# A graph kernel on one core: instruction order from a table of engine clocks, the second eight of a neighbour list from a code counted from the far end, and weighted slots summed by TensorE

## The chip, the cores and the metric

The kernel runs on one core of one Trainium2 chip. The metric is the time of one execution in microseconds on the device; the median of three runs without the profiler is given. A core has TensorE (PE in the profile: matmuls; PEld: its weight loads), VectorE (DVE), ScalarE (ACT), GpSimd (POOL), SyncE (SP: it only issues transfers here) and 16 DMA engines. Each engine works off its own instruction stream in order.

## The reference

There are 16 graphs of 1024 nodes with 64 features per node and a dense adjacency `adj` (16 x 1024 x 1024, float32). An entry is set with about 1.6% chance, and the diagonal is set. Four layers follow, each with a residual and a layer norm:

```
x = LN(x + tanh([x, adj @ x] @ W1 + b1) @ W2 + b2)          # layer 0
x = LN(x + (adj / max(rowsum(adj), 1)) @ x)                 # layer 1
for weights in (L2, L3):                                    # layers 2 and 3
    nb   = (adj > 0) without the diagonal;  m = nb.sum(-1)
    skip = ceil(m / 2) where m > 10                         # remove two neighbours of a node ...
    rem  = nb & ((rank + 1) % skip == 0);  rem |= rem.T     # ... and the reverse edges
    valid = (nb without rem) plus the node itself
    agg  = 0.25 q(0.25) + 0.5 q(0.5) + 0.25 q(0.75)         # quantiles, channel by channel, of x over the
    x    = LN(x + (relu((x + agg) @ V1 + c1) @ V2 + c2) * mask)   #   valid neighbours, interpolated
```

The quantiles are the heart: for every node, the features of its neighbours are gathered and sorted in each of 64 channels, and a few of the sorted slots are weighed and summed.

## The kernel before, in words

**Lists.** For each graph ("entry" `b`) the function `features` does layers 0 and 1 and makes `near`, the 0/1 adjacency in fp8. `lists` then works in steps. It counts the neighbours with TensorE (`pm`), finds ranks with a triangular matrix (`pr`), finds the two places to cut with ScalarE's Sign and an accumulator, marks them (`takes`), subtracts them and their transposes (`pv`), and counts what is left. It sorts the nodes by their count, so that a tile of 128 nodes has lists of like length: `order` is the permutation as a matrix. For each of the tiles 0 to 6 (`SIZES` 10, 11, 13, 14, 15, 17, 19 with the node itself) it multiplies `order` by the rest of `near` (`pk`), so that each neighbour appears as a code that falls with its new position, and takes the codes with VectorE: MAX8 gives the eight largest, MATCH_REPLACE8 strikes them out, MAX8 gives the next eight. The codes become indices `idx`.

**Gathering and sorting.** `ordered` permutes features and helper data. Graphs go in pairs; 16 rounds (`order_of_rounds`) are 8 pairs times the layers 2 and 3. For tiles 0 to 6 GpSimd gathers one list slot of 128 nodes with one indirect DMA (`gather`, L373) into a ring of `ROOM` = 60 slots for each of the pair's two graphs (`got_s`). `exchange` sorts the slots with VectorE min and max operations between `got_s` and `other`. `weigh` multiplies the wanted slots by weights on ScalarE (L850), adds them in a tree on VectorE and adds the two last into `agg`. The tile with the longest lists (half 21, half 33 slots) is not gathered: `fill` picks its neighbours with TensorE. For each slot a 0/1 mask `hot` is made from `place` (three of four by VectorE, the fourth by ScalarE at L808 and L809), and 24 matmuls (`pick`, L369) select rows into `pgk`, whose groups of four slots ScalarE copies to `got` (L800). `finish` does the small MLP of the round: transposes (`pt`, L886), two matmuls and a layer norm.

**Order.** VectorE, ScalarE and TensorE run exactly in the order in which the Python program emits their instructions (a manual schedule). All steps are generators. The class `Metered` adds up an estimated time for every VectorE instruction; a step yields a number, written by hand, of VectorE microseconds that should pass before it continues, and `Weave.catch_up`, called after every sorting operation, lets every due step emit its instructions:

```python
def step(self, work):
    try:
        work[0] = max(self.now() - work[2], work[0]) + work[3] * next(work[1])
```

Gathers are tried at the same moments (`fetch`), and only when the whole list of an entry is ready. All VectorE instructions of this part carry line 212 in the profile (the helper that counts them).

Of the kernel before, what the change touches and what calls it, by code (L numbers as in the profile page):

```python
# [12 lines left out]
F32 = mybir.dt.float32  # L13
# [16 lines left out]
KS = -(-(max(SIZES[:LISTED]) - 1) // 8) * 8  # L30
# [4 lines left out]
HOTS = 6  # L35
# [162 lines left out]
class Metered:  # L198


    def __init__(self, engine):
        self.engine, self.us = engine, 0.0

    def __getattr__(self, name):
        call = getattr(self.engine, name)

        def counted(*args, **kwargs):
            aps = [a for a in (*args, *kwargs.values()) if hasattr(a, "shape") and hasattr(a, "dtype")]
            size = max(prod(a.shape[1:]) for a in aps)
            fast = name == "tensor_scalar" and all(mybir.dt.size(a.dtype) == 2 for a in aps if prod(a.shape[1:]) > 1)  # L210
            self.us += 0.13 + size / (3840 if fast else 960)
            return call(*args, **kwargs)  # L212

        return counted
# [3 lines left out]
def adj_resnorm_kernel(ctx: ExitStack, tc: tile.TileContext, x, adj_t, nodemask, w01, b01, w02, b02,  # L218
# [10 lines left out]
    dve = Metered(nc.vector)  # L229
# [6 lines left out]
    make_identity(nc, ident)  # L236
# [16 lines left out]
    nc.gpsimd.iota(minus_k, pattern=[[-1, KW]], base=0, channel_multiplier=0, allow_small_or_imprecise_dtypes=True)  # L253
    one_f = const.tile([P, 1], F32, name="one_f")
# [27 lines left out]

    def per_row(ap, name):
        t = const.tile([P, C], F32, name=name)
        nc.sync.dma_start(t, ap.rearrange("(o c) -> o c", o=1).to_broadcast([P, C]))
        return t

    def column(ap, name):
# [4 lines left out]
        (weight(w21, "w21s"), column(b21, "b21c"), weight(w22, "w22s"), per_row(b22, "b22r")),  # L293
        (weight(w31, "w31s"), column(b31, "b31c"), weight(w32, "w32s"), per_row(b32, "b32r")),
# [87 lines left out]
    def settle(dst, y, chain):  # L382
# [4 lines left out]
        yield 2  # L387
# [3 lines left out]
        yield 9  # L391
        dve.reduce_sum(st[:, 2], dst, axis=AX.X)
        yield 1
        nc.scalar.activation(st[:, 3], st[:, 2], AF.Sqrt, bias=eps, scale=1.0 / C)
        yield 6
        dve.reciprocal(st[:, 0], st[:, 3])
        yield 1
        for t in range(NT):
            nc.scalar.activation(dst[:, t, :], y[:, t, :], AF.Copy, scale=st[:, 0, t : t + 1])
        yield 7  # L400

    def split(xc, parts, rest):

        yield 1
        nc.scalar.copy(parts[:, :, 0, :], xc)
        yield 6
        dve.tensor_sub(rest, xc, parts[:, :, 0, :])
        yield 1
        nc.scalar.copy(parts[:, :, 1, :], rest)
        yield 6  # L410
        dve.tensor_sub(rest, rest, parts[:, :, 1, :])
        yield 1
# [4 lines left out]
    def features(b, e):  # L417
# [11 lines left out]

        load(0)  # L430
# [4 lines left out]
        yield 8  # L435
        for h in range(NH):

            node_in = s.work.tile([P, HALF], F32, name="node_in", bufs=1)
            px = s.psum.tile([P, HALF], F32, name="px", tag="x", bufs=1)
            for q in range(G):  # L440
                nc.tensor.transpose(px[:C, q * P : (q + 1) * P], x_s[:, h * G + q, :], ident)
            for q in range(G):
                t = h * G + q
                for jt in range(NT):
# [4 lines left out]
                yield 5  # L449
                load(t + 2)  # L450
            yield 5
            nc.scalar.copy(node_in[C:], px[C:])
            yield 3
            nc.tensor.matmul(px[:C], w01s, node_in, start=True, stop=True)
            yield 9
            hid_t = s.work.tile([C, HALF], F32, name="hid_t", tag="node_in", bufs=1)
            nc.scalar.activation(hid_t, px[:C], AF.Tanh, bias=b01c)
            yield 3
# [3 lines left out]
            yield 10  # L462
# [3 lines left out]
        while b >= 2 and not entries[b - 2].packed:  # L466
            yield 2
        near = s.sets.tile([P, NT, N], F8, name="near", bufs=2)
        for h in range(NH):
            pa = s.psum.tile([P, G, C + 1], F32, name="pa", tag="x", bufs=1)  # L470
            for q in range(G):
                i = NT + h * G + q
                t = i - NT
                rows = slice(t * P, (t + 1) * P)
                for jt in range(NT):
                    nc.tensor.matmul(pa[:, q, :], adj[i][:, jt, :], x1[:, jt, :], start=jt == 0, stop=jt == NT - 1)  # L476
                yield 4
                dve.tensor_scalar(near[:, :, rows], adj[i], 0.0, None, op0=ALU.is_gt, saturate=False)
                dve.tensor_tensor(near[:, t, rows], near[:, t, rows], ident_b, op=ALU.is_gt, saturate=False)
                load(i + 2)  # L480
            yield 8
# [4 lines left out]
        e.near = near  # L486
        x2 = s.feat.tile([P, NT, C], F32, name="x2", tag="x_s", bufs=1)
        dve.tensor_add(y, y, x1[:, :, :C])
        yield from settle(x2, y, "x")
        while b and entries[b - 1].xs[0] is None:  # L490
            yield 2
# [4 lines left out]
    def lists(b, e, pace):  # L496

        while e.near is None:
            yield 2
        near = e.near  # L500

        st = s.work.tile([P, 6, NT], F32, name="nb_st", bufs=1)
# [3 lines left out]
        pm = s.psum.tile([P, N], F32, name="pm", tag="big", bufs=2)  # L506
# [3 lines left out]
        yield 12  # L510
        nc.scalar.copy(m, pm[:, :NT])
        yield 5
# [10 lines left out]
        for t in range(NT + 1):  # L523
            if t < NT:
                pr = s.psum.tile([P, N], F32, name="pr", tag="big", bufs=2)
                prs.append(pr)
# [5 lines left out]
            yield 1.2  # L532
            if t:
                for i in range(2):
                    junk = s.work.tile([P, N], F16, name="junk", tag="dist", bufs=3)
                    nc.scalar.activation(junk, prs[t - 1], AF.Sign, bias=lim[:, i, t - 1 : t], scale=-1.0,  # L536
                                         accum_out=cut_at[:, i, t - 1 : t])
            yield 3
        yield 5
# [5 lines left out]
        dve.tensor_scalar(off, off, 0.25, None, op0=ALU.mult)  # L545
        while b and not entries[b - 1].placed:
            yield 2
        takes = s.sets.tile([P, NT, N], BF, name="takes")
        dists = []
        for t in range(NT + 2):  # L550
# [3 lines left out]
            yield 1.3  # L554
            if t >= 2:
                dve.tensor_scalar(takes[:, t - 2, :], dists[t - 2], off[:, t - 2 : t - 1], None, op0=ALU.is_equal)
# [11 lines left out]
        yield 3  # L568
        for t in range(NT + 1):
            if t < NT:  # L570
                rows = slice(t * P, (t + 1) * P)
                pv = s.psum.tile([P, N], F32, name="pv", tag="big", bufs=2)
                pvs.append(pv.rearrange("p (c n) -> p c n", n=P))
# [7 lines left out]
            yield 1.2  # L581
            if t:
                nc.scalar.activation(left(t - 1), pvs[t - 1], AF.Relu, saturate=False)
# [31 lines left out]
        for t in range(NT):  # L615
            dve.tensor_scalar(order[:, t, :], slot, key[:, 2, t : t + 1], None, op0=ALU.is_equal)
            if t % 3 == 2:
                yield 2
# [795 lines left out]
```

## Time and profile before

| | |
|---|---|
| median of 3 runs | 5103.43 us (5102.24 to 5104.99) |
| profiled execution | 6960.85 us, of which 6959.1 us from the first to the last instruction |
| VectorE | 4338.6 us busy, 9272 instructions |
| GpSimd | 3219.1 us busy; 2944 gathers of 1045 ns and 128 stores of rows of 1060 ns |
| TensorE | 4047.0 us busy in 44,824 matmuls; mean granted clock 0.69 |
| ScalarE | 2838.3 us busy, 6388 instructions |
| DMA | 255.23 MB, mean 37 GB/s |

The profiled execution is much longer than a run without the profiler. A row of the costliest groups gives the line, the engine, the operation, output <- inputs, shapes and count, then busy us and mean ns, then the idle time of the engine just before these instructions and what ended it. A row of the waits gives who waited, for what, total us, times, and the longest.

### The profile page before, as it was taken

To read this page: it belongs to the slowest core of one execution; us is meant where nothing else is said; L and a number is where in the kernel's file an instruction comes from. 1 tells how busy PE (TensorE), PEld (TensorE's weight loads), DVE (VectorE), ACT (ScalarE), POOL (GpSimd) and SP (SyncE) were. 2 spreads that over 40 slices of the span, in tenths; PEclk is the share of its full clock that TensorE was granted. 3 is DMA by queue.
4 is the path that set the end of the run, shared out by engine and by line. 5 is a ranking of instruction groups with operands and counts; after the bars stand their busy time and mean duration, and the time that the engine had idled before them with its cause. 6 is when DMAs were issued, how large, how long until landed. Compare 5 with 4: busy or idle time off the path is not lost.

```text
span 6959.1 us, 112002 instructions
## 1 busy us (share of the span) xinstructions
PE 4047.0 (58%) x44824; PEld 2895.5 (42%) x44824; DVE 4338.6 (62%) x9272; ACT 2838.3 (41%) x6388; POOL 3219.1 (46%) x3168
## 2 busy tenths in 40 slices
PE   6757657386557665666666566665756563333243
PEld 5435435254334443444445344443534443223232
DVE  2446537577647668485665858566574767557575
ACT  4336335354344445344433535334353443223232
POOL 0342225625453545454454644455453645665551
PEclk8778777597668766767676667766667675555555
DMA  3111102111111111111111111111111100000100
GB/s 87 46 44 50 49 24 49 40 48 42 46 31 40 43 43 35 36 45 32 43 41 41 37 34 44 32 43 40 43 34 27 34 18 22 21 21 17 22 19 6
DMA packets 416527, 255.23 MB, mean 37 GB/s; under 512 B 104554, under 2 KB 366842, under 8 KB 415994
## 3 DMA queue, kind: packets, MB, share of 16 engines
q1 hardware_dynamic: 317690, 147.12, 7.7%
q0 software_dynamic: 98304, 100.86, 6.8%
q8 instruction: 352, 5.77, 0.3%
q14 instruction: 181, 1.48, 0.1%
HBM read 235.18 MB, written 12.59 MB: 36 GB/s over the span
## 4 chain that ended last, share of the span: by engine, by line
PE 34%; DVE 28%; issue 20%; another core or an unknown queue 8%; ACT 7%; POOL 1%; DMA 1%; DVEq 0%; ACTq 0%; POOLq 0%
PE pgk L369 11%; DVE other L212 11%; DVE got_s L212 7%; PE pk L640 6%; DVE got L212 5%; PE pa L476 4%; PE px L445 2%; PE ordered_x L369 2%; PE pr L530 1%; ACT got_s L850 1%; PE pk L632 1%; POOL got_s L373 1%; DVE hot L212 1%; PE pk L638 1%
## 5 line engine op out<-in xcount | busy, mean ns | idle before, releaser
L373 POOL DMA_INDIRECT got_s<-table,idx x2944 | 3075.3, 1045 | 3514.5 <-issue 784.3
L369 PEld LDWEIGHTS <-hot 128*128 128x128 bf16 x24576 | 1092.7, 112 | 1821.9 <-issue 1488.7
L369 PE MATMUL pgk<-x0p,hot 128*128 128x64 bf16 x12288 | 655.0, 212 | 694.6 <-issue 517.1
L369 PE MATMUL pgk<-x1p,hot 128*128 128x64 bf16 x12288 | 664.4, 216 | 646.5 <-issue 407.4
L800 ACT COPY got<-pgk 64x256 f32<-64x256 f32 x416 | 151.9, 365 | 1976.7 <-PE pgk L369 1352.4
L212 DVE TENSOR_SCALAR hot<-place 128x1024 bf16<-128x1024 f16 x768 | 332.0, 435 | 730.2 <-remote 518.2
L640 PE MATMUL pk<-near,order 128*128 128x512 fp8e4 x1792 | 495.9, 419 | 56.2 <-issue 54.0
L212 DVE TENSOR_TENSOR other<-got_s 128x512 f32<-128x512 f32 (+9 forms) x850 | 507.7, 608 | 29.8 <-ACT got_s L1035 15.3
L212 DVE TENSOR_TENSOR got_s<-got_s 128x512 f32<-128x512 f32 (+9 forms) x867 | 483.6, 560 | 18.4
L530 PE MATMUL pr<-steps,near 128*128 128x512 bf16 x1536 | 420.2, 436 | 96.8 <-ACT junk L536 72.5
L476 PE MATMUL pa<-x,adj_r 128*128 128x65 f32 x2048 | 359.7, 332 | 165.7 <-issue 156.9
L850 ACT ACTIVATE got_s<-got_s,wts 128x64 f32<-128x64 f32 x1568 | 393.8, 335 | 79.6 <-DVE got_s L212 70.7
L476 PEld LDWEIGHTS pa<-x,adj_r 128*128 128x128 f32 x2048 | 344.1, 251 | 177.5 <-issue 166.9
L212 DVE TENSOR_TENSOR got_s<-other 128x512 f32<-128x512 f32 (+9 forms) x731 | 401.2, 562 | 9.5 <-DVE other L212 1.5
L212 DVE TENSOR_TENSOR other<-other 128x384 f32<-128x384 f32 (+10 forms) x617 | 322.3, 522 | 17.1
L651 ACT ACTIVATE code<-pk 128x1024 f16<-128x1024 f32 x112 | 114.2, 1020 | 511.7 <-PE pk L640 344.5
L212 DVE MAX8 best<-code 128x8 f16<-128x1024 f16 x240 | 293.8, 1224 | 45.3 <-ACT code L651 32.3
L445 PE MATMUL px<-adj_r,x_s 128*64 128x128 f32 x2048 | 291.6, 299 | 47.4 <-issue 35.0
L640 PEld LDWEIGHTS <-order 128*128 128x128 bf16 x1792 | 167.3, 103 | 327.2 <-issue 197.4
L536 ACT ACTIVATE junk<-pr,nb_st 128x1024 f16<-128x1024 f32 x256 | 281.6, 1106 | 52.0 <-remote 21.8
L530 PEld LDWEIGHTS <-near 128*128 128x128 fp8e4 x1536 | 165.6, 110 | 327.9 <-issue 199.4
L809 ACT ACTIVATE hot<-hot,one_f 128x1024 bf16<-128x1024 bf16 x256 | 293.9, 1148 | 12.7 <-remote 4.4
(215 smaller groups left out, 7095.5 us busy)
## 6 DMA issues: line engine op xcount, KB each, us to landing
adj_r<-in_adj_dram SPq DMA_DIRECT2D x256, 512.0 KB
got_s<-table,idx POOLq DMA_INDIRECT x2944
x_s<-in_x_dram SPq DMA_DIRECT2D x16, 256.0 KB
table<-x2s SPq DMA_DIRECT2D x16, 256.0 KB
table<-x3s SPq DMA_DIRECT2D x16, 256.0 KB
out_dram<-agg,out_rows POOLq DMA_INDIRECT x128
table<-no_row SPq DMA_DIRECT2D x12, 0.2 KB
w01s<-in_L_gnn_W_dram SPq DMA_DIRECT2D x1, 32.0 KB
```

The source lines that it names most:

```text
L212: return call(*args, **kwargs)
L369: nc.tensor.matmul(dst, hot[:, c, :], parts[:, c, q, :], start=first and c + q == 0, stop=c == NT - 1 and q == 2)
L373: nc.gpsimd.indirect_dma_start(out=dst, out_offset=None, in_=tab, in_offset=bass.IndirectOffsetOnAxis(ap=rows, axis=0))
L445: nc.tensor.matmul(px[C:, q * P : (q + 1) * P], x_s[:, jt, :], adj[t][:, jt, :], start=jt == 0, stop=jt == NT - 1)
L476: nc.tensor.matmul(pa[:, q, :], adj[i][:, jt, :], x1[:, jt, :], start=jt == 0, stop=jt == NT - 1)
L530: nc.tensor.matmul(pr[:, h * HALF : (h + 1) * HALF], near[:, c, t * P : (t + 1) * P], steps[:, ONSET + h * HALF - c * P :][:, :HALF], star ...
L536: nc.scalar.activation(junk, prs[t - 1], AF.Sign, bias=lim[:, i, t - 1 : t], scale=-1.0, accum_out=cut_at[:, i, t - 1 : t])
L640: nc.tensor.matmul(cols, order[:, c, rows], left(c, slice(h * G, (h + 1) * G)), start=False, stop=c == NT - 1)
L651: nc.scalar.activation(codes[done], pks[done], AF.Relu, scale=float(N))
L800: nc.scalar.copy(got[rows, waiting[0] : waiting[0] + 4, :], waiting[1][rows])
L809: nc.scalar.activation(by_act, by_act, AF.Relu, bias=one_f, scale=-1.0)
L850: nc.scalar.activation(got[:, m, i, :], got[:, m, slot_id, :], AF.Copy, scale=e.wts[:, t, i : i + 1])
```

## The change

**Order.** `Metered` and all yielded numbers go. `Clocks` keeps one clock per engine and, for blocks of 128 bytes, when they were last written and read. Every emitted instruction (`Timed` wraps all engines) is priced, starts in this model once its engine is free and its inputs are there, and moves the clocks. A step yields nothing (it comes again 0.3 us after its last result, or polls every 0.5 us) or the model time at which it wants to go on; `Weave.run` always takes the earliest. Steps ask the model before they emit: `landed` (inputs written), `vacant` (buffer free), `big` (one of two PSUM buffers read out), `hot_room`. `fetch` and the sorting become steps of their own; a gather may be issued once its own tile is listed. `lists` is cut in two (`cuts` and `lists`); making the `hot` masks (`mark_picks`) is apart from the picking (`fill`); a finished tail list is sorted as soon as it is filled. For entries 0 to 3 `near` is marked in the first pass over the adjacency (layer 0) and not in the second.

```diff
-class Metered: ...
+class Clocks:
...
+    def put(self, engine, name, args, kwargs):
...
+        took, late = self.cost(engine, name, out, ins)
+        start = max(self.free[engine], self.now)
...
+                    start = max(start, end if by == engine else seen)
...
+        end = self.free[engine] = start + took
...
+        def run(self):
+            while self.works:
+                work = min(self.works, key=lambda w: (w[0], w[1]))
+                clocks.now, clocks.last = max(clocks.now, work[0]), 0.0
...
+                if at is None:
+                    at = clocks.last + SLACK if clocks.last else clocks.now + POLL
...
+    def landed(*aps):
+        while clocks.when(*aps) > clocks.now:
+            yield clocks.when(*aps) + SLACK
```

In `features` (where `first` is `b < 4`), `fetch`, `exchange` and `fill`:

```diff
+                if first:
+                    mark(t)
...
-            for i in range(1, SIZES[t]):
-                gather(got[:, m, i, :], ...)
+                for i in range(1, SIZES[t]):
+                    yield from quiet("POOL", 3.0)
+                    gather(got[:, m, i, :], ...)
...
         for is_max, d, v, i, j, to in usual[t]:
+            ins = view(pair[i], v), view(pair[j], v, d)
+            while max(clocks.free["DVE"], clocks.when(*ins)) > clocks.now:
+                yield max(clocks.free["DVE"], clocks.when(*ins))
...
-            weave.catch_up()
-            fetch()
+            yield clocks.now
...
+            while True:
+                at_least = max(clocks.when(hot), clocks.free["PE"] - (SLACK if k < 2 else 4.0), clocks.unused(pg) if place == 0 else 0.0)
+                if at_least <= clocks.now:
+                    break
+                yield at_least
```

Picks are copied out in groups of `GROUP` = 3 slots instead of 4; there are `HOTS` = 5 mask buffers instead of 6.

**Second eight.** ScalarE makes two codes of a tile instead of one: one that is large for the first neighbours, one that is large for the last. Lists of 9 to 16 neighbours need one MAX8 on each and no MATCH_REPLACE8; the list of 18 takes two on the near end and one on the far end. Where both cover a neighbour twice, a comparison drops the second.

```diff
-                    nc.scalar.activation(codes[done], pks[done], AF.Relu, scale=float(N))
+                    nc.scalar.activation(codes[done][0], pk, AF.Relu, bias=ends_of[:, 0:1], scale=2.0 * N)
+                    nc.scalar.activation(codes[done][1], pk, AF.Abs, bias=ends_of[:, 1:2], scale=2.0 * N)
+                    nc.scalar.activation(codes[done][1], codes[done][1], AF.Relu, bias=ends_of[:, 2:3], scale=-1.0)
...
-                size = -(-links // 8) * 8
-                for k in range(0, size, 8):
-                    dve.max(best[:, k : k + 8], rest)
-                    if k + 8 < size:
-                        dve.match_replace(rest, best[:, k : k + 8], rest, 0.0)
+                firsts = -(-(SIZES[done] - 1) // 8) - 1
+                for k in range(firsts):
+                    dve.max(best[:, k], near_end)
+                    if k + 1 < firsts:
+                        dve.match_replace(near_end, best[:, k], near_end, 0.0)
+                dve.max(best[:, 2], far_end)
...
+                dve.scalar_tensor_tensor(signed[:, most:links], best[:, 2, : links - most], signed[:, KS : KS + 1], rest,
+                                         op0=ALU.is_gt, op1=ALU.mult)
```

**Sums.** The weighted slots and the node's own features are summed by TensorE, which multiplies each by the identity and accumulates in `acc`, a strip of 128 columns in PSUM; one tile at a time (`adding`); the constant `HALVINGS` of the code below is 0, so that no add of the tree is left. The sum is transposed by this, so `finish` needs no transposes; ScalarE copies it to `agg`. The count of neighbours left now comes from the accumulator of the Relu that writes them, so a second ScalarE pass is gone.

```diff
-        while left > 2:
+        for _ in range(HALVINGS):
             more = left // 2
             dve.tensor_add(...)
             left -= more
-        if t < LISTED:
-            dve.tensor_add(agg[:, which, t, :], prods[:, :, 0, :], prods[:, :, 1, :])
...
+        while adding:
+            yield
+        adding.add(k)
...
+            for i in range(left):
+                nc.tensor.matmul(acc[own, rows], prods[:, i, :], ident[:, rows], start=i == 0, stop=False)
+            nc.tensor.matmul(acc[own, rows], e.xs[layer][:, at, :], ident[:, rows], start=False, stop=True)
         free.add((k, t, present))
         free.add((k, t))
+        yield
...
+            nc.scalar.copy(agg[own, at, :], acc[own])
+        adding.remove(k)
...
-        dve.tensor_add(agg, agg, xc)
...
-                nc.tensor.transpose(pt[:C, q * P : (q + 1) * P], agg[:, h * G + q, :], ident)
...
-                nc.scalar.activation(left(t - 1), pvs[t - 1], AF.Relu, saturate=False)
-                nc.scalar.activation(junk, left(t - 1), AF.Sign, accum_out=key[:, 4, t - 1 : t])
+                nc.scalar.activation(left(t - 1), pv, AF.Relu, accum_out=key[:, 4, t - 1 : t], saturate=False)
```

## The prediction

> **What bounds the kernel now.** I read the busy line first, then the costliest groups of VectorE and GpSimd, then their waits, then single stretches.
>
> The head of the page, the busy time of each engine:
>
> ```profile
> span 6959.1 us, 112002 instructions
> PE 4047.0 (58%) x44824; PEld 2895.5 (42%) x44824; DVE 4338.6 (62%) x9272; ACT 2838.3 (41%) x6388; POOL 3219.1 (46%) x3168
> ```
>
> Under the profiler no engine is full. But the median without it is 5103.43 us, 1857 us less than the profiled 6960.85 us, for the same instructions. Operations don't get shorter because nobody looks (a VectorE operation of 512 floats takes 687 ns here, and that is its slope and fixed cost, see below), so what is missing from the timed runs is idle time. In a timed run VectorE is then busy 4338.6 / 5103 = 85%, and at most 765 us idle.
>
> GpSimd looks lighter than it is. Its gathers, in order of time:
>
> ```profile
> 2058.42 0.94 POOL L373 DMA_INDIRECT got_s<-table,idx  x1 [0.31 <-issue]
> 2059.66 0.94 POOL L373 DMA_INDIRECT got_s<-table,idx  x1 [0.30 <-issue]
> ...
> 2083.10 1.39 POOL L373 DMA_INDIRECT got_s<-table,idx  x1 [0.31 <-issue]
> ```
>
> Start to start is 1.24 us although 0.94 is called busy: each gather brings 0.30 us of issue. With the mean of 1045 ns it is 1.345 us a gather. There are 2944 gathers and 128 stores of rows: 3072 x 1.345 = 4132 us, 81% of the timed run. So two engines share the bound, and each feeds the other. GpSimd's waits show how:
>
> ```profile
> POOL got_s L373 <- issue: 784.3, 2434, 25.7
> POOL got_s L373 <- DVE other L212: 764.3, 86, 87.9
> POOL got_s L373 <- DVE got_s L212: 676.1, 104, 29.5
> POOL got_s L373 <- ACT got_s L850: 617.9, 103, 23.3
> ...
> POOL got_s L373 <- DVE code L212: 193.7, 1, 193.7
> ```
>
> The 764, 676 and 618 us are gathers that wait for room in the ring: sort, weighing and adding of an older tile are not done. The last line is the start: the first gather goes out at 202.35 us. VectorE's own longest waits:
>
> ```profile
> DVE hot L212 <- remote: 518.2, 48, 61.7
> DVE y_m L212 <- PE pd L899: 241.1, 30, 28.5
> DVE hot L212 <- PE pgk L369: 200.7, 49, 19.9
> DVE deg L212 <- PE pa L476: 172.2, 14, 56.8
> ```
>
> These are waits of source order: a `hot` mask stands in VectorE's stream before a buffer is free, and sorts that could run stand behind it. TensorE is late there partly because of the profiler (`PEld L369 <- issue` 1595 us, `PE pgk L369 <- issue` 925 us, waits for nothing on record), which I take for most of the 1857 us.
>
> **What the Trainium skill says.** "VectorE: DVE Perf Modes", section on the TRN2 errata, gives a float32 `tensor_tensor` of N elements (N+151)/0.96 ns, 691 for 512; the trace has 687 to 691 and 292 for 128, so it agrees, and I price removed adds with it. "TensorE: Matmul & The Clock Gate", Part 1, has two clocks, 1.2 and 2.4 GHz; the trace agrees: 32 matmuls `px` L445 take 3.65 us (114 ns each) at one place, while 256 of `pt` L886 keep TensorE busy 55.5 us (217 ns each). "ScalarE: Activation LUTs", section on ACT_TABLE_LOAD, gives 280 + 0.833 N ns for an activation with a pointer bias, 1133 at 1024; the trace has 1144 and 1148 (`hot`), 1106 from PSUM.
>
> **The change part by part.** Counts are from the built instruction lists of both kernels.
>
> *Sums to TensorE.* VectorE loses 238 adds `got_s<-got_s` with 71,700 elements, (71,700 + 238 x 151)/960 = 112 us; 96 `got<-got` with 24,600 elements, 41; the 119 + 64 adds into `agg`, 31 + 3 + 14 = 48; 32 adds `agg+x` of 512, 22. The MLP's bias adds become 128 of half width, +10. Sum -213 us.
> TensorE gains 1792 float32 matmuls of 128 columns for seven tiles of a list (1568 slots, 224 own rows) and 928 of 64 columns for the tail: at 114 to 217 ns and half of it 204 + 53 to 389 + 101 us, less 256 transposes (29 to 56): +230 to +435 us on 4047. TensorE isn't the bound: its dense pieces run far below its mean (144 `ordered_x` in 4.20 us, 29 ns each; 24,576 `pgk` at that rate are 713 us, on record at 1319). Hidden beside VectorE, except for order, see the rivals.
>
> *Second eight from the other end.* MATCH_REPLACE8 goes from 128 to 16: 112 x (1209 + 92 ns for its value load) = -146 us. MAX8 stays 240. 112 small comparisons come, at 179 ns (a 128x8 row) +20. Sum -126 us. ScalarE pays: two more passes over 1024 per tile, 112 x (1106 + 1148 ns) = 252, 336 small copies at some 0.24 us 80, evacuations of the sums 50, copies by three instead of four 25; it loses 128 `junk` passes, -135, and the `o_t` copies, -37. About +240 us on 2838: 3080, 60 to 67% of any run forecast here, hidden.
>
> *VectorE in all:* -213 - 126 = -339 us, 4339 to 4000. GpSimd: nothing, 4132.
>
> *Order.* The order by summed VectorE time and written lags goes; each step is now placed when a table of engine clocks says that its inputs have landed. That moves everything, masks and matmuls included; mask making is now a task of its own, ahead of the matmuls. SP's adjacency loads and table writes move with it: the 256 loads wait for `px` in the SP queue (1805 us there), cost nothing where three buffers cover it, and would show as `px` waits on DMA if they came late; 1.2 us do today. Gathers may start per listed tile rather than per whole list. For entries 0 to 3 the `near` marks move to the first pass, so two stretches of 14 us (`pa` L476) leave the path to the first gather. On VectorE the marks stand before the adds of the first layer; those wait 0.7 us a mark, 8 x 0.7, which the loads cover. With five instead of six `hot` buffers a mask can wait one pick (24 matmuls of 29 ns, 0.7 us) more; from below nothing, from above 768 x 0.7 / 2 = 270 us if half did.
> The 765 us of idle time, split by the trace: some 150 of the first 200 us (VectorE is busy 50 us in the first two stretches of 100) and some 70 at the end (93 busy of the last 160) belong to the ends, 545 to the middle. I let the start fall to 110, the end to 60. For the middle nothing in the trace of before gives the answer: bounds 0 and 545, and I take half, 270.
>
> VectorE then ends at 4000 + 110 + 60 + 270 = 4440. GpSimd has its own sum: first gather at 165, 4132 of gathers, some 85 from the last gather to the end, 4382 with no stall at all. Two chains this even delay one another: the ring holds 60 slots, a round needs 99. I add 5% of the gathers, 200 us: **4580 us**. Against the profiled run: its VectorE was idle 2620 us, most of it the profiler's; the profiled span should fall by about the 339 us of work plus waits, to some 6100 to 6600, but I don't wager on that.
>
> **The rivals.**
> *Work alone.* The order gains nothing, since the waits only change their names: 5103 - 339 = 4764. For it: half the `hot` waits come from late TensorE, and order doesn't speed that. Against: y_m, deg, own waits are pure order.
> *Gathers alone.* The order is so good that GpSimd never stalls: 4132 + 202 + 100 = 4434, or less if a gather costs less unprofiled. For it: 2058 us of ring waits in the trace, which such an order aims at. Against: the ring keeps its size.
> *Slower: the one strip of sums.* All sums go through a single strip of PSUM, one tile at a time, and stand in TensorE's one stream behind `pk` groups and `pv` steps that wait for ScalarE (`PE pv L576 <- ACT near L583`: 143.6 us in 28 waits, up to 35.8). Ring room is given back only after the sum, so a gather waits for TensorE where it waited for an add of VectorE. There are 119 + 32 such sums. The gain of 339 us is gone once each holds the ring 339 / 151 = 2.2 us longer on the path; at 3 us it is 4764 + 453 = 5217. An add tree takes 213 / 151 = 1.4 us today, a sum of two members 16 x 0.217 = 3.5 us plus its place in the queue, so the point is within reach if the ring is the limit all the time and the order brings nothing.
> *No difference.* Less VectorE work is filled by waits for gathers and TensorE: 5100. That needs both engines idle at 20% with a better order, unlikely. That the change doesn't do what it says is ruled out by the instruction lists: the adds and 112 replacements are gone.
>
> **How the numbers follow.** Forecast 4580 (chance 0.43), work alone 4764 (0.24), gathers alone 4434 (0.20), slower by the strip 5217 (0.10), same 0.03. A measurement can tell about 0.2% here. Faster 0.87, same 0.03, slower 0.10. The range takes in the first three with the bounds of the middle's idle time and the `hot` buffers: from just under 4434 to 4764 plus half the 270, 4380 to 4900; 0.13 lies in the other two cases, and the rest beyond its ends.
>
> **What would show it.** VectorE busy 4000 +- 40 us on some 8,760 instructions; MATCH_REPLACE8 x16; gathers x2944 at the same 1.05 us; TensorE busy 4280 to 4480, ScalarE about 3080. The first gather before 170 us. `hot` waits of VectorE well below 730 us, and GpSimd's waits for `other`, `got_s` below 2058. If instead GpSimd waits mostly for the sums on TensorE, the strip has decided; if VectorE's busy time stays above 4200 my prices are wrong; if the busy time falls and the time doesn't, the order is.

## The result, and the profile after

The kernel after takes 5039.09 us (median of 4 runs, 5028.11 to 5056.69) beside 5103.78 us for the kernel before: a ratio of 0.9877 (95% interval 0.9848 to 0.9905), 65 us faster. The forecast was 4580 us, 459 us too low, and the result lies above the whole range of 4380 to 4900.

One thing is needed to read the numbers: the kernel before takes 5104 to 5106 us on some chips and 6988 to 7110 us on others. Its profile, of 6960.85 us, shows what chips of the second kind show; its times and the profile of the kernel after are those of the first kind.

This is the head of the page of the kernel after. The rows of digits show 40 equal slices of the span: tenths of busy time for three engines, and the granted TensorE clock in tenths of full speed.

```profile
span 5035.1 us, 123964 instructions
...
PE 3791.2 (75%) x50028; PEld 3000.9 (60%) x50200; DVE 4018.0 (80%) x8678; ACT 3079.9 (61%) x7175; POOL 3312.4 (66%) x3168
...
PE   6887988887888787888788777888878675563532
...
DVE  2568558897898978888888987988798888879593
...
POOL 0436217776377775777667675777757776777774
PEclk9989987898999888889899888888988887776765
```

The profiled execution took 5036.86 us, as long as the others, so profiling costs this kernel next to nothing. The work of two engines came out as forecast: VectorE 4018 us on 8678 instructions (4000 on 8760), ScalarE 3080 (3080). TensorE's 3791 us lie below the forecast of 4280 to 4480; that is at least in part the kind of chip, as a kernel run on both kinds shows below. VectorE is idle for 5035 - 4018 = 1017 us, where the forecast's sum for VectorE left it 440, and the 4580 us left it 580. TensorE, which was called "not the bound", is at least 70% busy in every slice from the 2nd to the 31st.

Rows of the costliest groups (busy us, mean ns; then the idle time before them):

```profile
L300 POOL DMA_INDIRECT got_s<-table,idx x2944 | 3165.2, 1075 | 1629.4 <-issue 509.9 <-DMA got_s<-table,idx 219.7 <-DVE other L300 179.8
L300 PE MATMUL pgk<-ident,got_s 128*64 128x128 f32 x3136 | 423.5, 311 | 226.8 <-ACT got_s L300 177.3 <-ACT got L300 46.3 <-ACT agg L300 3.0
L300 PE MATMUL pgk<-ident,got 128*64 128x64 f32 x1792 | 140.6, 254 | 180.1 <-ACT got L300 146.7 <-DVE takes L300 33.5
L300 ACT COPY agg<-pgk 128x128 f32<-128x128 f32 (+2 forms) x183 | 44.0, 240 | 200.5 <-PE pgk L300 199.6
L300 DVE MATCH_REPLACE8 code<-best,code 128x1024 f16<-128x1024 f16 x16 | 19.3, 1208 | 0.0
```

The replacements are 16, and the sums are on TensorE (`pgk<-ident`; the trace has two records for each of these float32 matmuls, 3136 for 1568 slots). GpSimd's stream is 3165.2 us of gathers, 139.2 us of stores and 3072 pauses of 0.30 us, 4226 us in all. In the other 809 us of the span GpSimd stands still, the start and the end included. Three long stalls come early (start and duration of a gather, in brackets how long GpSimd was idle before it, and what ended that):

```profile
179.44 1.13 POOL L300 DMA_INDIRECT got_s<-table,idx  x1 [170.78 <-PE pk L300]
368.36 0.94 POOL L300 DMA_INDIRECT got_s<-table,idx  x1 [66.53 <-DVE best L300]
580.25 0.97 POOL L300 DMA_INDIRECT got_s<-table,idx  x1 [91.82 <-DMA table<-x2s]
```

A little more than half of the 809 us, 436 us, falls in the first 750 us, while the first entries are listed one after another. The waits of VectorE and of TensorE in the kernel after (total us, times, longest):

```profile
DVE hot L300 <- PE pgk L300: 195.1, 152, 9.2
DVE other L300 <- DMA got_s<-table,idx: 97.0, 17, 16.1
DVE y_x L300 <- PE pd L300: 72.3, 15, 15.2
DVE place L300 <- PE pp L300: 62.4, 15, 10.4
DVE y_m L300 <- PE m_o L300: 59.0, 34, 10.4
```

```profile
PE pgk L300 <- ACT got L300: 459.9, 160, 31.8
PE pgk L300 <- ACT got_s L300: 177.3, 18, 26.2
PE pgk L300 <- ACT agg L300: 72.3, 46, 11.9
```

```profile
ACT got_s L300 <- DVE got_s L300: 307.3, 81, 25.3
```

VectorE waits for TensorE in four of its five rows, 389 us together, and 97 us for gathers. TensorE in turn stands at picks and sums until ScalarE has read a strip or weighed a slot, 710 us. And ScalarE's weighing waits for VectorE's sort, 307 us. Read so, no engine is late by itself; they hand over to each other in many short waits.

### The profile page after: what moved, and what is told of

It reads as the page before. It is cut to its first block, busy times and chain, and to the rows that moved or that the text cites. A ratio compares the mean times of both kernels' runs of the same rounds, so it can differ in the third digit from the quotient of the medians.

```text
span 5035.1 us, 123964 instructions
## 1 busy us (share of the span) xinstructions
PE 3791.2 (75%) x50028; PEld 3000.9 (60%) x50200; DVE 4018.0 (80%) x8678; ACT 3079.9 (61%) x7175; POOL 3312.4 (66%) x3168
## 5 line engine op out<-in xcount | busy, mean ns | idle before, releaser
L300 POOL DMA_INDIRECT got_s<-table,idx x2944 | 3165.2, 1075 | 1629.4 <-issue 509.9
L300 PEld LDWEIGHTS <-hot 128*128 128x128 bf16 x24576 | 902.5, 106 | 457.8 <-issue 265.7
L300 PE MATMUL pgk<-x1p,hot 128*128 128x64 bf16 x12288 | 488.7, 205 | 142.0 <-ACT got L300 76.0
L300 PE MATMUL pgk<-ident,got_s 128*64 128x128 f32 x3136 | 423.5, 311 | 226.8 <-ACT got_s L300 177.3
L300 PEld LDWEIGHTS pgk<-ident,got_s 128*64 128x64 f32 x3136 | 377.4, 156 | 262.5 <-ACT got_s L300 197.0
L300 PEld LDWEIGHTS <-order 128*128 128x128 bf16 x6912 | 349.2, 100 | 258.6 <-issue 96.4
L300 PEld LDWEIGHTS <-near 128*128 128x128 fp8e4 x4608 | 343.9, 101 | 212.6 <-issue 59.4
L300 DVE TENSOR_TENSOR got_s<-got_s 128x512 f32<-128x512 f32 (+10 forms) x629 | 371.8, 595 | 16.2
L300 ACT ACTIVATE code<-pk,ends_of 128x1024 f16<-128x1024 f32 x224 | 240.0, 1105 | 200.5 <-DVE best L300 101.5
L300 ACT ACTIVATE junk<-pr,nb_st 128x1024 fp8e4<-128x1024 f32 x256 | 284.3, 1111 | 62.9 <-PE pr L300 57.3
L300 ACT ACTIVATE hot<-place,minus_k 128x1024 bf16<-128x1024 f16 x256 | 292.7, 1143 | 42.6 <-PE pgk L300 36.4
```

## The experiments

There are four theories: **G**, the stream of gathers (4226 us and the start) sets the time; **V**, VectorE's stream sets it; **T**, TensorE's does (T2 in the expectations; T there means the late instructions of some chips); **C**, none alone: the time is a chain that runs through all of them, and each engine's work pays only for its share of that chain. G was my first reading of the profile after.

### Is it the profile that is slow? The kernel before once more

No edit. e1:

> The kernel before once more, for a second profile. If the 1857 us between its first profile (6959.1 us) and its timed runs are the profiler's doing in TensorE's instruction stream, this profile is again far above 5103 (6500 to 7100 us). If the first profile was a freak, this one lies within 1% of 5103, as the profile of the kernel after lies at its own timed runs.

e6:

> A profile of the kernel before on a chip where it takes 5100 us (on the other chip this is a third look at 7000 to 7110). VectorE busy 4340 as before, TensorE without waits for nothing. Theory G: GpSimd's gathers at about 1.37 us plus some 900 us of stalls. Theory V: GpSimd stalls often and evenly for ring room (over 900 us), VectorE busy 85%.

Measured: 7106.59 us beside runs of the same kernel with a median of 7109.62, and 7115.48 beside 7086.44. So a run of 7100 us isn't made by profiling: on these two chips every run is that long. The prediction's sentence that most of the 1857 us are the profiler's is false. Seven chips were used in the runs of this section; only one was used twice, and it was of the first kind both times. That the chip and not the occasion makes the difference is therefore likely, and not shown.

### The change once more

No edit; on a chip where before takes 5103.77 us.

> The kernel after itself, beside the kernel before on the same chip. Where the kernel before takes 5100 us, 5030 to 5060 us is expected by every theory. Where it takes 7110 us (TensorE's instructions come late there), theory G, which says that nothing but GpSimd counts, gives 5040 too; theory T (late TensorE instructions stall every engine, and this kernel has some 5200 matmuls more) gives 6900 to 7500.

Measured: 5051.05 us, ratio 0.9894 (0.9865 to 0.9923). The recorded result repeats.

### Fewer gathers, and the order alone, where TensorE's instructions come late

These runs were meant to tell G from V, but fell on chips where the kernel before takes 6990 to 7110 us. The edits: 420 gathers left out, in the kernel before and in the kernel after (two of each listed tile of the later lists; in the latter they are still priced, so that the order stays), and the kernel after with tree and single code restored, which leaves the new order.

```diff
                 for i in range(1, SIZES[t]):
+                    if n >= 14 and i <= 2:        # 420 gathers
+                        clocks.put("POOL", "indirect_dma_start", ...)   # only in the kernel after
+                        continue
                     gather(got[:, m, i, :], ...)
```

> The kernel before without two of the gathers of each tile and graph from the second round on (i = 1 and 2: 420 of 2944 left out, those slots keep old data). Theory G (GpSimd's stream of gathers sets the time): 420 x 1.35 us = 567 us less, 4540 (4480 to 4620). Theory V (VectorE's stream in its source order sets it, gathers have slack): over 4950.

> The kernel before without 420 of 2944 gathers (slots i = 1 and 2 from the second round on keep old data). Theory G: 4500 to 4600. Theory V: 4900 to 5100. (Where before takes 7110: 6634, as seen.)

> The kernel after without the same 420 gathers; they are still priced in its table of clocks, so every other engine's order is unchanged. Theory G: 420 x 1.378 = 579 us less, 4460 to 4560. Theory V: over 4900, since VectorE's work (4018 us) and its waits stay.

> The kernel after without the same 420 gathers, all else in the same order. Theory G: 579 us less, 4440 to 4600. Theory V: over 4850. (Where before takes 7110: 6980, as seen.)

> The kernel after without 420 of 2944 gathers, order unchanged. Where the kernel before takes 5100 us: theory G (GpSimd sets the time) 5050 - 579 = 4440 to 4600; theory V (VectorE and the order set it) over 4850. Where before takes 7100: 6980, as seen twice.

> The kernel after with both savings on VectorE undone (tree of adds instead of TensorE's sums, MATCH_REPLACE8 and one code per tile instead of two): new order with nearly the old work. Theory G: VectorE's 330 us more lie beside the gathers, 5000 to 5120. Theory V: VectorE's work comes on top, 5300 to 5400, and then the order alone would be a loss against 5103.

> The kernel after with both savings on VectorE undone (adds in a tree, MATCH_REPLACE8, one code). Theory G: the added 330 us of VectorE lie beside the gathers: 5020 to 5150. Theory V: 5300 to 5400. (Where before takes 7110: 7415, as seen.)

> The kernel after with both other parts undone: tree of adds and one code with MATCH_REPLACE8, so the new source order alone. If the two halves just add (e13: 43 us less than the kernel after, e14: 29 us more), it takes 5030 where the kernel before takes 5106, a ratio of 0.985: then the whole gain comes from the order, and 280 us less VectorE work bring nothing. If VectorE's stream set the time, it takes 5045 + 280 = 5320, slower than the kernel before. On a chip with late TensorE instructions the ratio was 1.043.

One more landed there: the kernel after with one slot of each sum, all others priced and left out.

```diff
             for i in range(left):
+                if i:
+                    clocks.put("PE", "matmul", (acc[own, rows], prods[:, i, :], ident[:, rows]), {})
+                    continue
                 nc.tensor.matmul(acc[own, rows], prods[:, i, :], ident[:, rows], start=i == 0, stop=False)
```

> The kernel after with one slot of each sum added by TensorE in place of all (1344 + 832 float32 matmuls left out but still priced, so that the order stays; its output is not the reference's). TensorE has some 390 us less to do, VectorE, ScalarE and GpSimd the same. Theory T2, TensorE's stream with the sums in it sets the time: 200 to 350 us less than 5045. Theory C, the order couples TensorE, VectorE and GpSimd, all near full, and each pays for its own waits: 40 to 120 us less. Theory V: less than 40.

| kernel | median us | kernel before there | ratio (95%) |
|---|---|---|---|
| e2 before, fewer gathers | 6634.35 | 7109.62 | 0.9328 (0.9287 to 0.9369) |
| e7 the same, another chip | 6654.42 | 7086.44 | 0.9379 (0.9349 to 0.9408) |
| e3 after, fewer gathers | 6980.27 | 7109.62 | 0.9823 (0.9779 to 0.9867) |
| e8 the same, another chip | 6976.95 | 7086.44 | 0.9851 (0.9834 to 0.9867) |
| e10 the same, a third | 6987.66 | 7084.21 | 0.9863 (0.9812 to 0.9913) |
| e4 order alone | 7414.77 | 7109.62 | 1.0429 (1.0384 to 1.0473) |
| e9 the same, another chip | 7405.07 | 7086.44 | 1.0446 (1.0424 to 1.0469) |
| e15 the same, a fourth | 7297.40 | 6988.22 | 1.0433 (1.0402 to 1.0465) |
| e16 after, one slot of each sum | 7304.42 | 6988.22 | 1.0437 (1.0402 to 1.0472) |

What is late there can be read in a line or two. TensorE's 64 small matmuls `ps`, in the kernel after on a chip of the first kind (e11 below), are one piece of 1.77 us:

```profile
335.08 1.77 PE L300 MATMUL ps<-own,order 128*128 128x3 f16 x64
```

In e16 the same kind of matmuls comes, in one such place, in groups of four, one about every 0.74 us, and nothing on record is waited for:

```profile
2516.86 0.25 PE L300 MATMUL ps<-own,order 128*128 128x3 f16 x4 [0.41 <-issue]
2517.60 0.25 PE L300 MATMUL ps<-own,order 128*128 128x3 f16 x4 [0.50 <-issue]
2518.35 0.24 PE L300 MATMUL ps<-own,order 128*128 128x3 f16 x4 [0.49 <-issue]
2519.08 0.25 PE L300 MATMUL ps<-own,order 128*128 128x3 f16 x4 [0.49 <-issue]
```

One kernel was profiled on both kinds: that of e3 is also that of e12 below, 6980 us here and 4968 us there. TensorE's weight loads for the picks, first in e3, then in e12 (`issue` is idle time for which nothing on record was waited for):

```profile
L300 PEld LDWEIGHTS <-hot 128*128 128x128 bf16 x24576 | 1043.8, 110 | 1461.2 <-issue 1278.6
```

```profile
L300 PEld LDWEIGHTS <-hot 128*128 128x128 bf16 x24576 | 900.1, 105 | 447.2 <-issue 264.7
```

TensorE is also busy for longer with the same work, 4314 us in e3 beside 3790 us in e12. It looks as if instructions reach TensorE late on these chips and all else waits; the traces don't show why. So no theory of the 5039 us can be judged here. The kernel after itself wasn't run there, and I don't know why chips differ, nor why e16 is slower than the kernel before. Two things stand: an order that gains by the sums below on one kind of chip loses on another (4.3 to 4.5%, three times), and fewer gathers take 432 to 475 us, 6% to 7%, off the kernel before (e2, e7). That is most of the 567 us that G expected: what a gather is worth depends on the kernel, on the kind of chip, or on both. In e3, e8 and e10 the change and the cut can't be told apart, as their base is missing.

### Each part undone, and fewer gathers, where before takes 5106 us

e11 is the kernel after itself, the base of the rest:

> The kernel after as it is, as the base of the three runs beside it. Where the kernel before takes about 5100 us: 5030 to 5060 with the gathers' stream at 4230 us plus about 800 us of stalls. Where the kernel before takes about 7090 us (TensorE's instructions come late there): theory T, all engines wait for TensorE, expects a ratio near 0.985 as well (about 6990); theory V, the source order sets it, expects 0.93 to 0.96 (6600 to 6800), because VectorE has 320 us less to do.

e12 is the edit of e3 again:

> The kernel after without 420 gathers (two of each listed tile of the lists from number 14 on: their output is not the reference's), everything else in the same order. Theory G, the stream of gathers sets the time: 420 x 1.378 = 579 us less than the kernel after on the same chip, 4400 to 4600 where that is 5040. Theory V, VectorE's stream sets it: less than 150 us. Theory T on a chip with late TensorE: less than 100 us.

e13 gives the adds back to VectorE down to two slots:

```diff
-        for _ in range(HALVINGS):
+        while left > 2:
```

> The kernel after with the sums' halvings back on VectorE (tree of adds down to two slots, then the matmuls). VectorE gets about 150 us of adds back. Theory G: they lie beside the gathers, but slow those that run beside them (1.10 instead of 0.945 us): -10 to +60 us against the kernel after. Theory V: +120 to +200 us.

e14 makes one code again (`scale=float(N)`, one Relu) and puts MATCH_REPLACE8 between the MAX8:

```diff
-                for k in range(firsts):
-                    dve.max(best[:, k], near_end)
...
-                dve.max(best[:, 2], far_end)
+                for k in range(0, size, 8):
+                    dve.max(best[:, k : k + 8], rest)
+                    if k + 8 < size:
+                        dve.match_replace(rest, best[:, k : k + 8], rest, 0.0)
```

> The kernel after with one code per tile and MATCH_REPLACE8 between the MAX8 again. VectorE gets about 126 us back, ScalarE loses about 330. Theory G: the middle stays; listing of the first four entries, which lies on the path to the first gathers, becomes longer or shorter by up to 20 us: -30 to +40 us against the kernel after. Theory V: +100 to +170 us.

| kernel | median us | to e11 | ratio to before (95%) |
|---|---|---|---|
| e11 after | 5045.16 | | 0.9888 (0.9872 to 0.9905) |
| e12 420 gathers less | 4967.99 | -77 | 0.9734 (0.9718 to 0.9750) |
| e13 adds back on VectorE | 5002.00 | -43 | 0.9796 (0.9780 to 0.9812) |
| e14 one code, replacements back | 5073.84 | +29 | 0.9941 (0.9925 to 0.9958) |

**G falls**: 420 gathers of 1.378 us (1.078 and the pause of 0.30), 579 us, are gone, and 77 us are gained. In e12 the gathers wait for the sort instead (total us, times, longest):

```profile
POOL got_s L300 <- DVE other L300: 491.9, 63, 76.0
```

That row was 179.8 us in the kernel after: a gather is spared, and the ring is still full until VectorE has sorted. **V alone falls** as well: e13 has more VectorE work and is faster. The busy times of e11 and of e13:

```profile
PE 3798.8 (75%) x50200; PEld 2996.6 (60%) x50200; DVE 4015.2 (80%) x8678; ACT 3079.6 (61%) x7175; POOL 3319.2 (66%) x3168
```

```profile
PE 3463.2 (69%) x46424; PEld 2639.9 (53%) x46424; DVE 4146.7 (83%) x9012; ACT 3073.6 (61%) x7165; POOL 3349.5 (67%) x3168
...
DVE 52%; PE 18%; ACT 16%; issue 5%; DMA 4%; POOL 4%; DVEq 0%; POOLq 0%; ACTq 0%
```

VectorE does 131 us more, TensorE 336 us less, and 43 us are gained: what these sums cost on TensorE is more than what the adds cost on VectorE. Unlike e12, e13 and e14 don't hold the order: what they add and leave out is priced as it is, so the table of clocks plans anew, and a part of the 43 and 29 us may be that. The mean granted clock is 0.82 in e13 and 0.85 in e11; what that costs isn't told apart. The last line is the chain that ended last in e13, by engine: VectorE has half of it, three engines the rest. (For e11 the profile follows the chain only through the last stores.) e13 beats both kernels: it is the change with most of its sums undone.

### Less VectorE work, and all three cuts at once

e17 leaves the exchanges of one member of the two largest listed tiles out, priced as before:

```diff
-            dve.tensor_tensor(view(pair[to], v, d if is_max else 0), *ins, ...)
+            aps = view(pair[to], v, d if is_max else 0), *ins
+            clocks.put("DVE", "tensor_tensor", aps, {})
+            if 4 < t < LISTED and view is cut_pair and pair[0].shape[1] == 2:
+                aps = [view(pair[to][:, :1], v, ...), view(pair[i][:, :1], v), view(pair[j][:, :1], v, d)]
+            whole.vector.tensor_tensor(*aps, op=ALU.max if is_max else ALU.min)
```

> The kernel after with the exchanges of the two largest listed tiles done for one of the two members alone (the other member's slots stay unsorted; its output is not the reference's). The work left out is still priced, so that the order stays. VectorE has 278,400 / 960 = 290 us less to do, no other engine changes. Theory V, VectorE's stream sets the time: 200 to 290 us less than the kernel after (4750 to 4850 where that is 5045). Theory C, the order couples three engines that are all near full: 60 to 150 us less. Theory T2, TensorE with its waits for ScalarE sets it: less than 40. On a chip with late TensorE instructions, where 420 gathers less and half the sums less brought nothing: within 1% of the ratio 0.985 of e8.

e18 makes the cuts of e12, e16 and e17 together:

> The kernel after with the three cuts at once and its order held: 420 gathers (GpSimd 579 us), the sums but for one slot (TensorE some 390 us), the exchanges of one member of the two largest listed tiles (VectorE 290 us); the output is not the reference's. The single cuts of GpSimd and VectorE brought 77 and 99 us; for TensorE's some 100 follow from e13 and e17 (335 us less TensorE for 131 us more VectorE work gave 43 us; VectorE pays 0.34 a us, so TensorE 0.26). If each engine pays its share whatever the others do, the sum: 276 us less, 4770. If the three hold one another, so that one cut is covered by the other two, more than the sum: 4450 to 4650. If the rest, the start, ScalarE and the hand-overs between engines, sets the time, less than the sum: 4800 to 4900. On a chip with late TensorE instructions: ratio 0.97 to 1.05, and nothing of this is told.

Measured beside kernels before of 5103.82 and 5106.47: e17 4946.48 us (ratio 0.9685, 0.9668 to 0.9702), e18 4783.41 us (0.9372, 0.9356 to 0.9387). To e11, which ran on another chip of the same kind, that is -99 and -262 us; medians of the kernel after itself lie between 5039 and 5051 us, so each such difference is known to some 10 us. The busy times of e17 and two of the waits of its VectorE:

```profile
PE 3791.9 (76%) x50200; PEld 2993.1 (60%) x50200; DVE 3733.9 (75%) x8678; ACT 3079.6 (62%) x7175; POOL 3254.9 (66%) x3168
```

```profile
DVE hot L300 <- PE pgk L300: 275.3, 214, 10.4
DVE y_m L300 <- PE m_o L300: 92.6, 52, 10.4
```

VectorE has 281 us less to do. 99 us come out at the end, and the rest became idle time: most of all in front of the masks that wait for TensorE's picks (from 195 to 275 us), then of the MLP (59 to 93). By e17 **T alone falls** too, for it expected less than 40 us of a cut on VectorE; and V expected 200 to 290.

The busy times of e18:

```profile
PE 3434.6 (72%) x45848; PEld 2612.8 (55%) x45848; DVE 3728.7 (78%) x8678; ACT 3074.9 (64%) x7175; POOL 2821.7 (59%) x2748
```

The three cuts together bring 262 us, close to the sum of 276 put down beforehand. Had each cut been small because the other engines cover it, removing the cover too would have brought more than the sum. The sum isn't measured throughout: TensorE's cut alone ran only where its instructions come late (e16), and its 100 us of the 276 are an estimate from e13. As far as that estimate holds, each engine has a share in one long chain, the same whether the others are lightened or not:

| engine | cut | work removed | gained | share (gained per us removed) |
|---|---|---|---|---|
| GpSimd | e12 | 579 us | 77 us | 0.13 |
| VectorE | e17 | 281 us | 99 us | 0.35 |
| TensorE, from e18 | 262 - 77 - 99 | 364 us | 86 us | 0.24 |
| TensorE, from e13 | 43 + 0.35 x 131 | 336 us | 89 us | 0.27 |
| ScalarE, from e14 | 0.35 x 133 - 29 | 271 us | 18 us | 0.07 |

Only the first two rows were measured by a cut in one engine alone (e17 also shortens the mean gather by 23 ns). The others follow by subtraction, TensorE's twice with like results, though both ways suppose that shares add; ScalarE's 18 us are hardly more than the uncertainty. A share is that of the work which was left out, not of every us of the engine. This is theory C, the only one of the four that the runs leave.

## Why the prediction was wrong, point by point

**Two engines "share the bound".** Wrong: there are at least three, and none of them bounds. The step that failed is "TensorE isn't the bound ... Hidden beside VectorE": the added TensorE work was put at nothing. A us of it costs 0.24 to 0.27 us here, by the subtractions above; that it costs more than it saves is measured by e13. TensorE's busy time in the profile of before was no guide: 58% there, where its instructions seem to come late, and 75% in the profile after.

**The price of VectorE's and ScalarE's work was right, its worth was not.** *Work alone* took 339 us of VectorE off the end one for one. At 0.35 each they would bring some 119. Two of the parts could be priced by undoing them: together they save VectorE 131 + 133 = 264 us, worth 92; the sums charge TensorE 336 us, worth 89, and the second code charges ScalarE 271 us, worth 18. The sums thus lose 43 us and the second eight gains 29; of the work called hidden, only ScalarE's part nearly was. TensorE's price was too low as well: the two rows of `pgk<-ident` above, 423.5 and 140.6 us, are 564 us for the slots alone, where the forecast has 257 to 490 for slots and own features together. Its 114 ns is what one of the two records of such a matmul takes in a dense run, and a matmul takes both. Its 217 ns for `pt` isn't a reading of the slower clock either: in the same trace a group of four of these takes 0.60 us at one place and 1.04 us at another.

**The order** brought the rest, if the parts add: 5045.16 - 43.16 + 28.68 = 5030.7 us for the order and what comes with it, 75 us below the kernel before. That is by subtraction; the order alone ran only where TensorE's instructions come late. The forecast wanted 184 us from it (4764 to 4580), and 523 us in the whole.

**Idle time of VectorE.** In the sum 4000 + 110 + 60 + 270 the last term is the one that failed most: idle time is 1017 us, not 440. In the stretches that the prediction used, the first 200 us hold 136 us of it (63.8 us busy), the last 160 us hold 80 (80.3 busy), and the middle 801 instead of 270. The bounds of the middle, "0 and 545", took the idle time of before as the most that could be left. The profile after has more than that: with some 320 us of work gone, idle time rose from the 765 us of the prediction to 1017, as e17 shows on a smaller scale (281 us less work, 99 us gained). The split was read in the profile of before and set against a median of 5103; but trace and median came from different kinds of chip. I saw the gap of 1857 us, and wrote most of it off as the profiler's. The halving of the middle was a guess, and half of the gain forecast hung on it.

**GpSimd's sum** was 4382, and 200 of stalls on top. Where nothing else is waited for, a gather starts every 1.375 us in the mean, not 1.345 (94 us in all); the first goes out at 179 us instead of 165, and the stalls after it are some 600 us. A correct sum wouldn't have helped: e12 shows that its length isn't what sets the end.

**The rivals.** *No difference*, which had 0.03, came closest: 5100, beside 5039 measured. It was called unlikely because it "needs both engines idle at 20%"; VectorE is idle for 20% of the span, and GpSimd stands still for 16%. *The slower strip* had part of the mechanism and a wrong size: sums on TensorE do lose time, 43 us net and not 453. Its way through the ring isn't what the trace shows: GpSimd waits 91.8 us for `pgk`, picks or sums, and more for listing and sorting. *Gathers alone*, my first reading afterwards too, is refuted by e12. Waits for `hot` did fall, from 730 to 207 us in the row of its group, and GpSimd's waits for `other` and `got_s` too, as foreseen; but the two profiles are of different kinds of chip, and how much of the fall is the order's isn't told apart. The prediction's last sign, "if the busy time falls and the time doesn't, the order is" at fault, pointed wrong: by the sums above the order gains, and the sums on TensorE lose.

**The start.** In the kernel after, the first graph's rows are stored at 1487 us, and in e12, e17 and e18 at 1465, 1477 and 1446: the three cuts hardly touch the first 30% of the span (that of the gathers begins only with the second round). From there to the store of the twelfth graph (4430 us in e11) e18 gains 200 us. A start that lists four graphs more quickly wasn't tried.

## What to carry to other kernels

When the profiled execution and the median differ by a third, as here, the profile may belong to another situation than the time: settle that before adding up anything. In a kernel whose engines hand over to one another in a fixed order, busy time moved from one engine to another isn't removed. Measure what a us is worth on each engine, by leaving some of its work out with the order held, and compare the whole cost on both sides: us of work times what one of them is worth. Here 131 us of adds on VectorE, though the dearer engine per us, cost less than the 336 us of float32 matmuls that take their place, and the kernel with the adds takes 5002 us.

## What the runs showed of the hardware that I had not expected

- The same program took 5104 to 5106 us on some chips and 6988 to 7110 on four others; one kernel profiled on both kinds kept TensorE busy for 3790 us on the first and 4314 us on the second, and in traces from the second TensorE waits much longer with no wait on record, in one place with matmuls in groups of four about every 0.74 us. The cause is open.
- A gather takes longer the busier VectorE is. With VectorE 55% busy (e16) the mean is 1017 ns, with 80% (after) 1075, in e17 with 75% it is 1055:

```profile
L300 POOL DMA_INDIRECT got_s<-table,idx x2944 | 2992.8, 1017 | 3989.9 <-DVE other L300 1385.2
```

```profile
L300 POOL DMA_INDIRECT got_s<-table,idx x2944 | 3107.3, 1055 | 1610.9 <-issue 502.5
```

Sorted by what VectorE runs beside them, the gathers of the trace after take 944 ns in the mean where VectorE is idle throughout (271 gathers), and, where one kind of instruction lies beside at least nine tenths of the gather, 944 beside MAX8 (113), 1061 beside a tensor_scalar (79) and 1112 beside a tensor_tensor (221; half of these take less than 960). The Trainium skill, "SBUF — State Buffer", section "Who interferes with whom", says that a VectorE instruction with two SBUF inputs contends with a GpSimd instruction that reads SBUF. That a tensor_tensor lengthens a gather and MAX8, with one input, doesn't agrees with it. The tensor_scalar has one tensor as input and isn't covered by that sentence, and that SBUF access is the cause isn't shown by any run.
